# A bottleneck with local self-attention and a bottleneck with a 3x3 convolution: image 0's first 1x1 convolution in seven block products for eight

## The chip, the cores and the metric

The kernel runs on one core of a Trainium2 chip. The metric is device time in microseconds (us); the time given is the median of three runs. A separate execution is recorded by the hardware profiler. Five engines run their own instruction streams and meet at semaphores: TensorE (PE, with its weight loads PEld), VectorE (DVE), ScalarE (ACT), GpSimd (POOL) and SyncE (SP). SP, ACT and POOL also issue DMA transfers.

## The reference

Two residual blocks on x of 16 images, 1024 channels, 32x32 pixels, all in f32:

```
h = relu(bn(conv1x1(x, w_conv1)))                 # 1024 -> 256 channels
q, k, v = relu(bn(wq h)), relu(bn(wk h)), bn(wv h)
attn = softmax over the 9 neighbours of  q . (unfold3x3(k) + pos_h + pos_w)   # 32 heads of 8 channels
h = relu(bn(sum over 9 neighbours of attn * unfold3x3(v)))
x = relu(bn(conv1x1(h, w_conv3)) + x)             # 256 -> 1024, residual
y = relu(bn(conv1x1(x, w1)));  y = relu(bn(conv3x3(y, w2)))
out = relu(bn(conv1x1(y, w3)) + x)
```

The batch norms of the second block have means and variances; those of the first are a scale and a bias.

## The kernel before

An image is 8 chunks of 128 channels by 1024 pixels. A PE product multiplies 128x128 weights with 128x512 data (half the pixels) into a PSUM bank; in the profile one such f32 product is two rows. PSUM holds four tiles of two banks ("ps"), handed out in turn, so that a new tile waits for whoever reads the one four tiles earlier.

The stages of PE stand in a list, in order (line 1026): `P0 P1 P2 P3 C4 F0 Q4 V4 F1 P5 P6 F2 P7 F3 C8 Q8 W0 V8 ...`. C is an image's first convolution (`first_conv`), Q its queries and keys with the position products, V its values (P is C, Q and V in a row), F the fused second half of the first block with the first convolution of the second, W a 3x3 convolution of four images in Winograd form, U and S the last convolution. S, for the last four images, already uses seven block products for eight (`change`, `Quad`, `late_weights`).

- **First convolution** (`first_conv`, `reduce_part`, L389): for each of eight chunks, four products (two output halves by two pixel halves) are summed in two PSUM tiles; two ACT instructions (L1095) then make the hidden tile h. Weights w1 come in two pieces of 512 KB, through `more_weights`.
- **Loads of x** (`more_loads`, L361): image 0's chunk 0 comes in two halves on ACT's queue, chunk 1 also on ACT's; all else on POOL's queue. An x tile is freed, and a later one loaded into it, when its products are done.
- **Projection** (`project`): a key k or a value v is written by ACT (L488) into the padded tile kp, and SP stores it to DRAM (L500), in stage Q or V, at the place in SP's order where it is computed. q goes to DRAM on POOL's queue (L548). The position products (L521) are summed in one tile, which ACT copies to `by_offset` (L529) and POOL stores. `relay` loads all of it back with one head in each partition.
- **Side work** (`Side`): a string of words, ORDER, one for each part of a stage, says what is recorded on DVE and ACT beside that part: j a step of an attention, e its exponentials, f a step of other work, m a load of relayed data, a the relu of an attention's result, w the relu of a Winograd result. Engines run in the order recorded.
- **The f work of the opening**: `winograd_weights` makes the 3x3 filters' Winograd form U: for each of two input halves three 128x768 passes on ACT and six on DVE (from the taps g, loaded by `load_taps`, L272), then six "sets" (`along`) of four ACT and six DVE instructions of 128x256, each of which fills a tile u (L283 to L293), stored by SP to uw (L305). u lies in the pool "h", five tiles that the hidden tiles and q share. `scale_weights` multiplies w3 and u3 by their batch norm scales (L255), after `load_scaled` and `scale_rows` have loaded weights and scales on POOL's queue.
- **Winograd stage** (`winograd_conv`, L822): 18 groups of 8 products. Each needs one weight load U on SP's queue (L132, five rooms) and one V load on POOL's queue; V was stored by SP (L787) from DVE's transform of the hidden images.

[...]

## Time and profile before

| | us |
|---|---|
| median of three runs (2362.63 to 2368.56) | 2364.83 |
| the profiled execution | 2362.54 |
| its span | 2360.8 |
| PE busy | 2349.4 |
| DVE busy | 2154.3 |
| ACT busy | 916.6 |
| POOL busy | 490.2 |

The granted PE clock averages 0.999. Image 0's first convolution takes PE from 4.83 to 33.94 us, its Q and V stages end at 57.35, image 1's first convolution at 85.16. Stage W0 begins at 664.81. The DMA engines move 292 GB/s on average and some 400 GB/s in the first 30 us.

To read the profile: a row of PE in order of time gives start, length, what it is and, in brackets, the idle time before it with what ended that. In lists of waits, the numbers are the total, the count and the longest. Matmuls overlap by 0.16 us in their modelled ends, so that a short wait inside a run of rows doesn't show as idle time; it shows in the starts of the runs.

### The profile page before, as it was taken

The page shows a single profiled execution, that of the slowest core. Times are in us where ns is not written, and L with a number is a line of the kernel's source. Part 1 is how long each engine was busy: PE and PEld are TensorE (multiplying, and loading weights), DVE is VectorE, ACT ScalarE, POOL GpSimd, SP SyncE. Part 2 cuts the span into 40 slices and gives each one's busy share as a digit, 9 for nine tenths or more (in the row PEclk, how much of TensorE's full clock was granted, in tenths as well). Part 3 has the DMA queues.
Part 4 walks back from the last instruction along what each step waited for, and adds up shares of the span by engine and source line. Part 5 has one row for each costly group of instructions (what it writes and reads, how often), then busy time and mean ns, then how long its engine had stood idle before and what let it go on. Part 6 is the DMA issues. An engine that isn't in the chain of part 4 may idle for free.

```text
span 2360.8 us, 18840 instructions
## 1 busy us (share of the span) xinstructions
PE 2349.4 (100%) x6252; PEld 1140.7 (48%) x6252; DVE 2154.3 (91%) x1770; ACT 916.6 (39%) x873; POOL 490.2 (21%) x900
## 2 busy tenths in 40 slices
PE   9999999999999999999999999999999999999998
PEld 4444444444475444444466444444467444444844
DVE  4999999999989999999999999999989999976686
ACT  3323342324122574443122574324222464344266
POOL 2212121212121231111121232111111231111132
PEclk9999999999999999999999999999999999999999
DMA  9968687878797998687898998688788996699888
GB/s 365 368 219 301 245 288 250 284 273 271 262 350 248 341 395 304 217 266 231 265 313 271 328 391 318 221 277 290 262 288 272 335 378 241 213 343 313 314 310 294
DMA packets 295568, 691.63 MB, mean 293 GB/s; under 512 B 20784, under 2 KB 165168, under 8 KB 286768
## 3 DMA queue, kind: packets, MB, share of 16 engines
q0 software_dynamic: 119888, 471.14, 54.9%
q1 hardware_dynamic: 174864, 217.93, 28.6%
q10 hardware_dynamic: 720, 1.36, 0.2%
q8 instruction: 50, 0.82, 0.1%
q14 instruction: 46, 0.38, 0.0%
HBM read 415.32 MB, written 275.03 MB: 292 GB/s over the span
## 4 chain that ended last, share of the span: by engine, by line
PE 91%; DVE 5%; DMA 3%; ACT 0%; issue 0%; POOL 0%; SPq 0%; DVEq 0%; ACTq 0%; POOLq 0%
PE ps L389 34%; PE ps L421 31%; PE ps L475 12%; PE ps L822 9%; PE ps L1263 4%; DVE acc L677 1%; DMA uw<-u 1%; DMA g<-in_u2t_dram 1%; DVE acc L695 1%; PE ps L521 1%; DMA v<-v 1%; DVE v L751 0%; DMA V__2_2534<-v 0%; DMA pos<-by_offset 0%; DVE z L848 0%
## 5 line engine op out<-in xcount | busy, mean ns | idle before, releaser
L389 PE MATMUL ps<-result,u 128*128 128x512 f32 x1024 | 457.8, 592 | 0.0
L421 PE MATMUL ps<-a,w 128*128 128x512 f32 x1024 | 457.7, 592 | 0.0
L389 PE MATMUL ps<-x,w 128*128 128x512 f32 x1024 | 442.9, 593 | 1.0 <-DMA x<-in_x_dram 0.9
L677 DVE TENSOR_TENSOR acc<-e,bnv 128x2048 f32<-128x2048 f32 x144 | 327.4, 2283 | 17.8 <-ACT e L659 14.7
L421 PE MATMUL ps<-y,u 128*128 128x512 f32 x768 | 331.1, 592 | 0.0
L620 DVE TENSOR_TENSOR prod<-qc,bnk 128x2048 f32<-128x2048 f32 x144 | 324.0, 2287 | 1.8
L440 ACT ACTIVATE result<-ps,par 128x1024 f32<-128x1024 f32 x128 | 142.4, 1113 | 458.1 <-PE ps L421 391.6
L389 PEld LDWEIGHTS ps<-x,w 128*128 128x128 f32 x1024 | 194.7, 190 | 246.5 <-issue 243.7
L389 PEld LDWEIGHTS ps<-result,u 128*128 128x128 f32 x1024 | 194.4, 190 | 245.3 <-issue 238.1
L421 PEld LDWEIGHTS ps<-a,w 128*128 128x128 f32 x1024 | 194.6, 190 | 244.9 <-issue 243.5
L695 DVE TENSOR_TENSOR acc<-acc 128x2048 f32<-128x2048 f32 x128 | 293.4, 2292 | 4.4
L421 PEld LDWEIGHTS ps<-y,u 128*128 128x128 f32 x768 | 145.9, 190 | 183.3 <-issue 181.0
L475 PE MATMUL ps<-h,wqk 128*128 128x512 f32 x512 | 222.4, 592 | 0.4 <-ACT h L1095 0.4
L441 POOL DMA_DIRECT2D r<-result x128 | 68.7, 537 | 596.6 <-ACT result L440 592.4
L625 DVE TENSOR_TENSOR prod<-prod 128x2048 f32<-128x2048 f32 (+1 forms) x80 | 166.1, 2077 | 2.2
L475 PEld LDWEIGHTS ps<-h,wqk 128*128 128x128 f32 x512 | 97.1, 190 | 123.2 <-issue 111.2
L440 ACT ACTIVATE result<-ps,bn_sh 128x1024 f32<-128x1024 f32 x96 | 106.7, 1112 | 102.5 <-PE ps L421 96.8
L1095 ACT ACTIVATE h<-ps,par 128x1024 f32<-128x1024 f32 x32 | 38.4, 1202 | 260.0 <-PE ps L389 260.0
L412 ACT ACTIVATE ps<-s 128x1024 f32<-128x1024 f32 x128 | 131.2, 1025 | 15.6 <-DMA s<-in_x_dram 13.1
L488 ACT ACTIVATE kp<-ps,par 128x1024 f32<-128x1024 f32 x64 | 77.3, 1209 | 149.5 <-PE ps L475 120.1
L361 POOL DMA_DIRECT2D x<-in_x_dram x126 | 67.0, 533 | 274.2 <-PE ps L389 205.3
L845 ACT ACTIVATE z<-ps 128x1024 f32<-128x1024 f32 x48 | 49.1, 1024 | 179.1 <-PE ps L822 124.4
(372 smaller groups left out, 2653.8 us busy)
## 6 DMA issues: line engine op xcount, KB each, us to landing
s<-in_x_dram POOLq DMA_DIRECT2D x128, 512.0 KB, 5.8
r<-result POOLq DMA_DIRECT2D x128, 512.0 KB, 4.6
x<-in_x_dram POOLq DMA_DIRECT2D x126, 512.0 KB, 5.2
out_dram<-result POOLq DMA_DIRECT2D x125, 512.0 KB, 7.1
r<-r POOLq DMA_DIRECT2D x111, 512.0 KB, 7.4
v<-v SPq DMA_DIRECT2D x96, 408.0 KB, 4.9
U<-uw SPq DMA_DIRECT2D x60, 512.0 KB, 5.2
bnk<-kp SPq DMA_DIRECT2D x32, 680.0 KB, 7.1
```

What stands on the lines that cost most here:

```text
L389: nc.tensor.matmul(ps[n][:, halves(half)], wt[:, c % (NC // 2), n * P : (n + 1) * P], src[:, halves(half)], start=(c == first), stop=(c == ...
L412: nc.scalar.activation(ps, loaded.pop((self.kind, self.b, o)), AF.Identity)
L421: nc.tensor.matmul(self.ahead[o][:, halves(half)], pieces[key][:, n, o % (NC // 2) * P :][:, :P], self.src[:, n, halves(half)], start=Fals ...
L440: nc.scalar.activation(to_, ps, RELU, bias=self.shift(o), scale=1.0)
L475: nc.tensor.matmul(ps[:, halves(half)], pieces[key][:, m, at : at + P], h[:, m, halves(half)], start=(m == 0), stop=(m == NW - 1),)
L488: nc.scalar.activation(dst, src, func, bias=col(f"L0_conv_{name}_b", n), scale=col(f"L0_conv_{name}_s", n),)
L620: nc.vector.tensor_tensor(by_row(t[:, two]), by_row(qc), kc[:, :, i : i + JROWS, j : j + W], ALU.mult)
L625: nc.vector.tensor_add(u[:, :, 0:4], u[:, :, 0:4], u[:, :, 4:8])
L677: nc.vector.tensor_tensor(by_row(dst), rows(e[:, k, :]).unsqueeze(1).to_broadcast([P, HEAD_DIM, JROWS, W]), vc[:, :, i : i + JROWS, j : j ...
L695: nc.vector.tensor_add(acc, acc, t)
L822: nc.tensor.matmul(acc[i][:, at, :, n, :], pieces[key][:, m, at, n * P : (n + 1) * P], v[:, at, :, m * (TILES + TR) :][:, :, :TILES], star ...
L1263: nc.tensor.matmul(ps, w, by, start=i in (1, 7), stop=True, skip_group_check=True)
```

## The change

Image 0's first convolution runs as `first_conv_of_seven`. Chunks are taken in pairs; with output halves and pixel halves each pair is a 2x2 by 2x2 block product, made with seven products for eight. DVE forms, for each pair, three sums of x halves t1 to t3 in rooms that the attention uses later, and t4 in place of a half of x; and for each piece of w1 four sums of weights s1 to s4 (`sums_of_weights`). The seven results lie in seven PSUM banks of four tiles; `combine` adds them with one ACT copy and seven DVE additions into h, and four ACT relus of 128x512 finish h.

Image 0's x comes as halves, on ACT's and SP's queues, in the order of need, with the first half of the second w1 piece on ACT's queue. Two lent rooms (of tags qc and bnk) hold the u tiles of sets 2 and 3. In `at_first`, four chunks of x go ahead of the second piece of w1; batch norms and the position table follow part 6 of the convolution, `load_scaled` its part 1, `scale_rows` the start of image 0's V stage. ORDER has the f steps of the opening later, the first attention's steps accordingly, and five pairs or so of single steps exchanged later on (the attention's steps in W0 among them).

SP's stores of k are recorded in a list (`put_off`) and issued at once, except in a Q stage followed by W0, which is image 8's: there they go out after part 3 of W0.

```diff
@@ more_weights
         if of[1] == 0 and name == "w1":
-            for part in (slice(0, 1), slice(1, k)) if half == 0 else (slice(0, k),):
-                nc.sync.dma_start(view[:, part], src[:, part])
+            for part, by in (
+                ((slice(0, 2), nc.scalar), (slice(2, k), nc.sync))
+                if half
+                else ((slice(0, 1), nc.sync), (slice(1, k), nc.sync))
+            ):
+                by.dma_start(view[:, part], src[:, part])
@@ winograd_weights
+        lent_rooms = {2: ("qc", JPIX), 3: ("bnk", HALO)}
+
         def along(m, i, row):
-            t = hpool.tile([P, 2 * HW], F32, tag="h", name="u")[:, : NI * WID]
+            if 6 * m + i in lent_rooms:
+                tag, width = lent_rooms[6 * m + i]
+                t = apool.tile([P, HEAD_DIM, width], F32, tag=tag, name="u").rearrange("p d w -> p (d w)")
+            else:
+                t = hpool.tile([P, 2 * HW], F32, tag="h", name="u")
+            t = t[:, : NI * WID]
@@ more_loads
-            by = nc.scalar if loads[0] in (("x", 0, 0), ("x", 0, 1)) else nc.gpsimd
-            for part in (halves(0), halves(1)) if loads[0] == ("x", 0, 0) else (slice(None),):
-                by.dma_start(t[:, part], src[:, part])
+            if (kind, b) == ("x", 0):
+                for part, by in ((halves(0), nc.scalar), (halves(1), nc.sync if c else nc.scalar)):
+                    by.dma_start(t[:, part], src[:, part])
+            else:
+                nc.gpsimd.dma_start(t, src)
@@ project, halo
-                nc.sync.dma_start(
-                    room[n], AP(block.tensor, block.offset, [block.ap[0], [JROWS * PW, NJ], [1, HALO]])
-                )
+                block = AP(block.tensor, block.offset, [block.ap[0], [JROWS * PW, NJ], [1, HALO]])
+                put_off.append(lambda to=room[n], block=block: nc.sync.dma_start(to, block))
+                if name != "bnk" or not stages[now[0] + 1 : now[0] + 2] or stages[now[0] + 1][:2] != FIRST_WINO:
+                    catch_up()
@@ new functions
+    def sums_of_weights(half):
+        s = weight_sums["all"]
+        a = pieces[piece("w1", half)].rearrange("p (q m) (n o) -> p m n q o", m=2, o=P)
+        s1, s2, s3, s4 = (s[:, i, 2 * half : 2 * half + 2] for i in range(4))
+        a11, a12, a21, a22 = a[:, 0, 0], a[:, 1, 0], a[:, 0, 1], a[:, 1, 1]
+        nc.vector.tensor_tensor(s1, a21, a22, ALU.add)
+        nc.vector.tensor_tensor(s2, s1, a11, ALU.subtract)
+        nc.vector.tensor_tensor(s4, a12, s2, ALU.subtract)
+        nc.vector.tensor_tensor(s3, a11, a21, ALU.subtract)
+    def first_conv_of_seven(b):
...
+            nc.vector.tensor_tensor(t1, one[:, halves(1)], one[:, halves(0)], ALU.subtract)
+            if pair % 2 == 0:
+                sums_of_weights(pair // 2)
+            by[1] = a[:, 0, :P], one[:, halves(0)]
+            by[5] = sums_of(0), t1
+            product(1)
+            if pair < last:
+                product(5)
+            yield
+            two = loaded.pop(("x", b, 2 * pair + 1))
+            t4 = one[:, halves(1)]
+            nc.vector.tensor_tensor(t2, two[:, halves(1)], t1, ALU.subtract)
+            nc.vector.tensor_tensor(t3, two[:, halves(1)], t4, ALU.subtract)
+            nc.vector.tensor_tensor(t4, t2, two[:, halves(0)], ALU.subtract)
+            by[2] = a[:, 1, :P], two[:, halves(0)]
+            by[3] = sums_of(3), two[:, halves(1)]
+            by[4] = a[:, 1, P:], t4
+            by[6], by[7] = (sums_of(1), t2), (sums_of(2), t3)
+            for i in (2, 3, 6, 7, 4) if pair < last else (2, 6, 5, 3, 7, 4):
+                product(i)
...
+    def combine(b, banks):
+        h = hidden[b] = hpool.tile([P, NW, HW], F32, tag="h", name=f"h_{b}")
+        c11, c12, c21, c22 = (h[:, n, halves(half)] for n in range(NW) for half in range(2))
+        p1 = u2 = u3 = c22
...
+        nc.scalar.activation(p1, banks[1], AF.Identity)
+        nc.vector.tensor_tensor(c11, banks[2], p1, ALU.add)
+        relu(0, 0, c11)
+        nc.vector.tensor_tensor(u2, banks[6], p1, ALU.add)
+        nc.vector.tensor_tensor(c12, banks[5], u2, ALU.add)
+        nc.vector.tensor_tensor(c12, banks[3], c12, ALU.add)
+        relu(0, 1, c12)
+        nc.vector.tensor_tensor(u3, banks[7], u2, ALU.add)
+        nc.vector.tensor_tensor(c21, u3, banks[4], ALU.subtract)
+        relu(1, 0, c21)
+        nc.vector.tensor_tensor(c22, banks[5], u3, ALU.add)
+        relu(1, 1, c22)
@@ at_first
         warm_up()
         more_weights()
+        more_loads(4)
+        more_weights()
         more_loads()
         nc.scalar.dma_start(par, params)
         more_weights()
-        norms()
         load_taps(0)
-        more_weights()
         load_taps(1)
         more_weights()
         member_table()
         nc.gpsimd.memset(kp, 0.0)
-        load_scaled()
-        scale_rows()
-        position_table()
+        hooks["conv1", 0, 1] = load_scaled
+        hooks["wino", 0, 3] = catch_up
+
+        def prepare():
+            norms()
+            position_table()
+
+        hooks["conv1", 0, 6] = prepare
+        hooks["v", 0, 0] = scale_rows
```

## The prediction

> **What bounds the kernel now.** I read the page first, then TensorE's (PE's) own waits, then its instructions in order of time over the first 110 us, then the chain of waits, and last the DMA issues of the sync engine (SP) around the only large wait.

> ```profile
> span 2360.8 us, 18840 instructions
> PE 2349.4 (100%) x6252; PEld 1140.7 (48%) x6252; DVE 2154.3 (91%) x1770; ACT 916.6 (39%) x873; POOL 490.2 (21%) x900
> ```

> PE is busy all but 11.4 us of the span, so a change can win only by giving PE fewer products or by removing some of its waits. PE's waits, longest in total first (engine and line, what it waited for, us in total, times, longest):

> ```profile
> PE ps L822 <- DMA V__2_2534<-v: 1.5, 1, 1.5
> ...
> PE ps L822 <- issue: 1.0, 1, 1.0
> PE ps L389 <- DMA x<-in_x_dram: 0.9, 1, 0.9
> PE ps L475 <- ACT h L1095: 0.4, 1, 0.4
> ```

> Some waits don't show there, because the ends of matmuls are modelled. They show in PE's rows in order of time (start, length):

> ```profile
> 4.83 3.95 PE L389 MATMUL ps<-x,w 128*128 128x512 f32 x8
> 9.67 24.27 PE L389 MATMUL ps<-x,w 128*128 128x512 f32 x56 [0.89 <-DMA x<-in_x_dram]
> 34.30 14.00 PE L475 MATMUL ps<-h,wqk 128*128 128x512 f32 x32 [0.36 <-ACT h L1095]
> 48.27 2.18 PE L521 MATMUL ps<-q,pos 64*32 64x512 f32 x16
> 50.38 7.13 PE L475 MATMUL ps<-h,wv 128*128 128x512 f32 x16
> 57.35 27.97 PE L389 MATMUL ps<-x,w 128*128 128x512 f32 x64
> 85.16 13.90 PE L475 MATMUL ps<-h,wqk 128*128 128x512 f32 x32
> ```

> Two rows are one product of the program. Undisturbed, 64 rows take 27.47 us (later stages in the chain of waits), so a product costs 27.47/32 = 0.858 us. Image 0's first convolution took 34.30 - 4.83 = 29.47 us for 32 products: 2.0 us of it is waiting. Next, 34.30 to 57.35 is 23.05 us, while the same work undisturbed is 13.73 + 1.02 + 6.97 = 21.72: 1.33 us went at the position products, whose queries (q) left ACT late. Image 1's convolution took 85.16 - 57.35 = 27.81, that is 0.34 us of waiting. The chain of waits says for what:

> ```profile
> 40.57 17.04 DMA uw<-u
> ...
> 58.35 0.92 ACT by_offset L529
> 59.31 26.02 PE ps L389 x60
> ```

> The second sum of image 1 needs the PSUM tile that by_offset (L529) empties, and by_offset stood on ACT behind the filter transform, which waited for its stores uw<-u. VectorE (DVE) waits 14.7 us for those stores in the first 80 us and is then busy over 98% of nearly every stretch up to 660 us.

> **Products.** 28 for 32 in image 0: -4 x 0.858 = -3.43 us of PE work.

> **When the first convolution ends.** Before, image 0's second half-chunk landed about 5.65 us (PE waited for it until 5.72), while three queues moved data; after, two queues hold only what image 0 needs, in order. ACT's first two halves (0.52 MB) with as much from SP are 1.05 MB, and the DMA windows (0.55 MB by 4 us, then 0.41 MB per us) give 5.2 us. I take 5.5. The second product needs t1 (128x512 SBUF add on DVE, 0.69 us in the last stage's rows) and s1 (128x256, 0.42 us): 5.5 + 0.1 + 0.69 + 0.05 + 0.42, with 0.2 to load weights, is 6.95 us. Chunk 1 completes at 1.57 MB, 6.5 to 6.9 us, and t2, t3, t4 at 8.85, 9.55, 10.25 lie ahead of their products (9.5, 10.4, 11.25). From then on data lead: all 5.24 MB are in by 16 us. T = 6.95 + 27 x 0.858 = 30.1 us, between 29.6 (no wait beyond the halves) and 31.5 (chunk 1 at 8 us). [...] The trace: three queues together moved 391 to 414 GB/s from 4 us on. [...]

> The DVE adds 16 x 0.69 + 8 x 0.42 + 7 x 0.69 = 19.2 us in 31 instructions. They lie in 5.5 to 31.7 us, where DVE was idle until 21.05 save for norms (3.2 us, now within the third pair, 5 us ahead of its use). The final sums run between the last products: the last two relus (0.69 us on ACT) end at T + 1.55 and T + 2.3, and the key product needs them at T + 1.72 and T + 2.57. So the 0.36 us wait goes, and the next stage starts at 30.2 for 34.30: **-4.1 us**.

> **What comes late after it.** The filter transform starts on DVE at 31.7 instead of 21.05 (on ACT, 18.7), and by_offset is still behind five of its sets on ACT. A set takes 2.65 us (DVE rows 27.30, 29.95). On ACT the order is now: both q, sets 1 to 3, the second key (1.2 us), sets 4 and 5, three 128x768 passes (0.75 us apart), by_offset. Counting from T: the second q leaves ACT at 11.7, set 1 runs on DVE from 12.2, set 5 from 22.8, its last ACT step ends at 23.2, the passes at 25.5, by_offset at 26.5. Image 1's second sum wants its tile at 0.1 + 21.72 + 1.72 = 23.5. PE waits **3.0 us**, where it lost 1.67 before (1.33 + 0.34): +1.3. From the other side: if ACT ran without these hold-ups the wait would be 0, and each us of a late uw store in set 4 or 5 adds one. The lent rooms make that unlikely: set 4 needs the store of set 0, issued at 40.7 and due at 50; it took 12 us before, with image 1's x still loading. Image 1's convolution thus ends 4.1 - 1.3 = 2.8 us sooner.

> **The rest of the opening.** The w3/u3 loads, row and scales move behind later steps on POOL: the loads behind pair 0's end (about 11.3 us, two x loads first), row/scales behind pc's load. The four scale products on DVE follow the first logits. Logits start at about T + 46.8 = 76.9 (before 81.4, after a transform ending 79.5); scales are needed at 81.4 and should land near 82, hidden or up to 3 us of DVE. DVE then stands 0 to 3 us ahead of before. Its next hold, the tree of L641 at 575.88, waited 2.79 us for by_offset of a later image, so small lateness vanishes there. The attention of image 1 has about 3.5 us to spare before PE's 309.8. par, the taps and wqk go behind x on SP: wqk is used at 30.2, the taps at 31.7, and by 0.4 MB per us (shared with POOL) they are in by 23. Cost 0; uncovered, each us late is one of PE.

> **The put-off stores.** SP in order of time around PE's longest wait:

> ```profile
> 654.84 0.59 SPq L500 DMA_DIRECT2D bnk<-kp  x1
> 655.52 0.55 SPq L132 DMA_DIRECT2D U<-uw  x1
> 665.13 0.36 SPq L500 DMA_DIRECT2D bnk<-kp  x1
> 665.59 22.32 SPq L132 DMA_DIRECT2D U<-uw  x7
> ```

> The second store waited 9.0 us for ACT, and behind it stood the weight load for the fifth group of products, whose 14.7 us end at 680.29; PE went on at 680.41 instead of 678.89. The page blames a V load, but that V belongs to the next group. After the change the weight load goes out as soon as the 16 key/query products end (before: 663.8), 1.7 us sooner, with 1.39 MB (3.5 us at 0.4 MB per us) less ahead. It would land near 676: **-1.5 us**, bounds 0 and -1.5. The stores now stand before the ninth weight load, which is issued near 679, took 12.0 us and is used at 694.3 (692.8 after): the same bytes are ahead of it as before, and 1.9 us are left. No V write of image 8 comes before 733. The later shuffles of single steps (two relus, one vh, one pair of logits) are hidden: they move ACT or DVE work between neighbours of the same stage. Cost 0; uncovered, one step of 1 to 4.5 us.

> **Sum.** -4.1 + 1.3 - 1.5 = **-4.3 us**. The profiled run took 2362.54 (span 2360.8 and 1.7 around it), 2.3 under the median of 2364.83; its like would be 2358.2, and against the median **2360.5 us**. The bound between change and none, 0.3%, is 7.1 us.

> **Rivals.**
> - *by_offset isn't late* (image 1's convolution keeps no wait). For: ACT is busy under half of that stretch. Against: my step-by-step count. Then -4.1 - 1.67 - 1.5 = -7.3: 2357.5.
> - *The put-off is worth nothing:* the next group waits instead. For: the following V load (issued 670.64) also landed near 680.3, and its weights at 682.96 against a need of 682.4. Against: the bytes ahead are gone. -2.8: 2362.0.
> - *DVE becomes the bound:* the four-deep ring of u rooms waits for its stores, and scales are late. DVE has nothing to spare from 80 to 660 us, so lateness reaches PE as soon as the cushions (2.8 us at L641, 3.5 before image 1's attention) are spent. For: 9.4 MB of u stores in 36 us, beside 8 MB of others, are 0.48 MB per us, above the 0.4 seen. It decides when the logits start 11 us later than before, at 92: about +7, 2372.

> **How the numbers follow.** Likeliest 0.45 (2358.5 to 2362.5), by_offset in time 0.30, put-off worthless 0.15, DVE late 0.10. Of the second, 0.27 lie beyond 7.1 us; of the last, 0.07. So faster 0.27, same 0.66, slower 0.07. The range, 2355.5 to 2367, takes in the first three with a measurement's 2 us, and small lateness of DVE.

> **What would show it.** PE's key products starting near 30.2; a gap of about 3 us soon after image 1's convolution begins (near 52), released by by_offset; logits at 77 to 80; no wait at the fifth group of the first Winograd stage. Wrong if PE waits in pairs 0 to 3, if DVE's waits for uw exceed 10 us, or if a new wait appears at 310 us.

## The result

The kernel after the change takes 2361.51 us in the median of 22 executions (2358.49 to 2363.45), the kernel before 2364.82 us (22 executions, beside it). The ratio is 0.9986, with a 95% interval of 0.998 to 0.9992: 3.3 us faster, within the 0.3% that the prediction called no change. The two profiled executions are equal (2362.54 before, 2362.59 after): the one of before lies 2.3 us under its median, the one of after 1.1 above. So the first question to the traces is where the 4.7 us that this execution had won by 52 us went again.

The page of the kernel after, its span and busy times:

```profile
span 2360.9 us, 18891 instructions
PE 2346.8 (99%) x6244; PEld 1139.6 (48%) x6244; DVE 2172.5 (92%) x1801; ACT 917.9 (39%) x876; POOL 487.2 (21%) x894
```

PE is busy 2.6 us less, not the 3.43 of four products: a slower stretch, below, is counted as busy. PE's waits after (what it waited for, us in total, times, longest):

```profile
PE ps L402 <- ACT by_offset L548: 2.7, 1, 2.7
PE ps L842 <- issue: 2.5, 1, 2.5
...
PE ps L842 <- DMA U<-uw: 1.1, 1, 1.1
PE ps L493 <- ACT h L1182: 0.3, 1, 0.3
PE ps L1142 <- DVE bnk L1115: 0.2, 1, 0.2
```

The waits for x and for V__2 are gone. Four others are new or longer. PE in order of time (start, length; idle time before in brackets); L1142 is a product of the seven, L402 is the old L389, L493 the old L475, L842 the old L822:

```profile
4.83 1.83 PE L1142 MATMUL ps<-x,w 128*128 128x512 f32 x2
6.83 1.12 PE L1142 MATMUL ps<-qc,bnk 128*128 128x512 f32 x2 [0.18 <-DVE bnk L1115]
...
30.11 2.06 PE L493 MATMUL ps<-h,wqk 128*128 128x512 f32 x4
32.45 12.28 PE L493 MATMUL ps<-h,wqk 128*128 128x512 f32 x28 [0.27 <-ACT h L1182]
...
52.65 1.88 PE L402 MATMUL ps<-x,w 128*128 128x512 f32 x4
57.18 27.71 PE L402 MATMUL ps<-x,w 128*128 128x512 f32 x60 [2.65 <-ACT by_offset L548]
84.73 13.90 PE L493 MATMUL ps<-h,wqk 128*128 128x512 f32 x32
```

Read against the rows of before: the key products start at 30.11 for 34.30 (-4.19), image 1's convolution at 52.65 for 57.35 (-4.70), but it ends at 84.73 for 85.16 (-0.43). Of the 4.27 lost in it against before, 2.81 are the wait for by_offset (the 2.65 of the row and the 0.16 by which modelled ends overlap). ACT makes that copy right behind the passes of the filter transform:

```profile
55.39 0.83 ACT L295 ACTIVATE g<-g 128x768 f32<-128x768 f32 x1
56.13 1.00 ACT L548 ACTIVATE by_offset<-ps 128x1024 f32<-128x1024 f32 x1
```

Another 1.80 are lost in the 60 rows behind the wait, which take 27.55 us (84.73 - 57.18) where 60 undisturbed rows take 25.75; before, image 1's convolution lost 0.34 in all. The windows of that stretch show why (busy time of PE, PEld, DVE, ACT, POOL with their counts, then the granted PE clock, the DMA share and GB/s):

```profile
56.00:58.00 2.00, 0.82 (x2) 0.53 (x3) 1.90 (x3) 2.00 (x6) 0.58 (x1) 0.91 1.08 293
58.00:60.00 2.00, 2.00 (x3) 0.78 (x3) 1.86 (x3) 0.35 (x2) 2.00 (x5) 0.50 1.07 415
60.00:62.00 2.00, 2.00 (x5) 0.73 (x4) 1.91 (x4) 0.00 (x0) 1.39 (x3) 0.74 1.08 268
62.00:64.00 2.00, 2.00 (x6) 0.94 (x5) 1.83 (x6) 0.46 (x2) 1.01 (x2) 1.00 0.81 311
```

The granted clock is 0.50 from 57.64 to 61.06 us: PE counts as busy, but the windows hold 3 and 5 rows in 2 us instead of 6. That costs half of 3.4 us, 1.7.

The 0.43 us stays until stage W0, which begins at 664.37 for 664.81. There and in W12, the last Winograd stage:

```profile
678.29 3.62 PE L842 MATMUL ps<-V__2_2504,U 128*128 128x256 f32 x16
...
693.32 3.69 PE L842 MATMUL ps<-V__1_2630,U 128*128 128x256 f32 x16 [1.05 <-DMA U<-uw]
...
2182.68 3.62 PE L842 MATMUL ps<-V__0_8347,U 128*128 128x256 f32 x16
...
2202.63 3.69 PE L842 MATMUL ps<-V__2_8425,kp 128*128 128x256 f32 x16 [2.52 <-issue]
```

The fifth group of W0 waits no more (1.52 before), the ninth now waits 1.05. From the first Winograd product to image 8's v products are 63.56 us (727.93 - 664.37) for 64.54. W12 begins 1.56 us sooner (2182.68 for 2184.24), but its sixth group starts at 2202.63 for 2202.69: it waited 2.52 for 1.02. "Issue" hides what it waited for: its V load was issued at 2190.99 and took 11.5 us to land, so at 2202.5; before, 2192.86 and 9.7, also near 2202.5. There what was left of this execution's gain was given back. The sync engine's queue (SP) around W0:

```profile
653.93 21.42 SPq L136 DMA_DIRECT2D U<-uw  x6
675.45 1.22 SPq L519 DMA_DIRECT2D bnk<-kp  x2
678.49 18.88 SPq L136 DMA_DIRECT2D U<-uw  x6
```

The put-off stores go out at 675.45, between the weight loads.

### The profile page after: what moved, and what is told of

Same layout as the page of the kernel before. It is cut to its first block, busy times and chain, and to the rows that moved or that the text cites. A ratio compares the mean times of both kernels' runs of the same rounds, so it can differ in the third digit from the quotient of the medians.

```text
span 2360.9 us, 18891 instructions
## 1 busy us (share of the span) xinstructions
PE 2346.8 (99%) x6244; PEld 1139.6 (48%) x6244; DVE 2172.5 (92%) x1801; ACT 917.9 (39%) x876; POOL 487.2 (21%) x894
## 4 chain that ended last, share of the span: by engine, by line
PE 98%; DMA 1%; DVE 0%; ACT 0%; issue 0%; ACTq 0%; DVEq 0%
PE ps L402 36%; PE ps L434 33%; PE ps L493 14%; PE ps L842 10%; PE ps L1379 4%; PE ps L1142 1%; PE ps L540 1%; DMA U<-uw 1%; DMA x<-in_x_dram 0%; DVE u L294 0%; DVE u L291 0%; ACT g L288 0%; DVE g L292 0%; ACT g L287 0%; ACT result L1409 0%
## 5 line engine op out<-in xcount | busy, mean ns | idle before, releaser
L402 PE MATMUL ps<-result,u 128*128 128x512 f32 x1024 | 457.8, 592 | 0.0
L402 PE MATMUL ps<-x,w 128*128 128x512 f32 x960 | 416.4, 594 | 2.7 <-ACT by_offset L548 2.7
L402 PEld LDWEIGHTS ps<-result,u 128*128 128x128 f32 x1024 | 194.4, 190 | 245.1 <-issue 238.4
L402 PEld LDWEIGHTS ps<-x,w 128*128 128x128 f32 x960 | 182.9, 191 | 233.7 <-issue 229.7
L493 PE MATMUL ps<-h,wqk 128*128 128x512 f32 x512 | 222.8, 593 | 0.3 <-ACT h L1182 0.3
L493 PEld LDWEIGHTS ps<-h,wqk 128*128 128x128 f32 x512 | 97.0, 190 | 123.4 <-issue 110.5
```

The lines of the kernel that those rows point to most:

```text
L402: nc.tensor.matmul(ps[n][:, halves(half)], wt[:, c % (NC // 2), n * P : (n + 1) * P], src[:, halves(half)], start=(c == first), stop=(c == ...
L493: nc.tensor.matmul(ps[:, halves(half)], pieces[key][:, m, at : at + P], h[:, m, halves(half)], start=(m == 0), stop=(m == NW - 1),)
```

## The experiments

Each kernel was timed beside the kernel before on the same chip; its ratio to that is given with the 95% interval. "The stretch" is that from the first Winograd product of W0 to image 8's v products.

| kernel | median us (n) | ratio to before | image 1's conv. ends | the stretch |
|---|---|---|---|---|
| changed kernel | 2361.51 (22) | 0.9986 (0.998 to 0.9992) | 84.73 | 63.56 |
| the same again | 2361.04 (20) | 0.9982 (0.9975 to 0.9988) | 83.46 | 64.35 |
| offset_early | 2356.24 (5) | 0.9966 (0.9953 to 0.9978) | 80.63 | 63.29 |
| the same again | 2357.37 (6) | 0.9971 (0.996 to 0.9983) | 80.51 | 63.70 |
| half_ahead | 2358.59 (8) | 0.9976 (0.9965 to 0.9986) | 82.70 | 65.24 |
| two_ahead | 2358.5 (20) | 0.9975 (0.9969 to 0.9982) | 81.62 | 62.97 |
| late_copy | 2364.76 (12) | 0.9997 (0.9989 to 1.0006) | 87.00 | 66.71 |
| eight | 2362.24 (13) | 0.9993 (0.9985 to 1.0001) | 86.71 | 62.26 |
| early_eight | 2358.32 (12) | 0.998 (0.9972 to 0.9989) | 82.83 | 62.60 |
| no_put_off | 2363.95 (12) | 0.9996 (0.9987 to 1.0004) | 83.69 | 67.05 |
| stores_later | 2360.77 (18) | 0.9983 (0.9976 to 0.999) | 84.75 | 64.34 |
| early_act_stores | 2364.87 (21) | 1.0003 (0.9997 to 1.001) | 80.56 | 70.98 |
| early_w12_queue | 2360.99 (21) | 0.9987 (0.998 to 0.9993) | 80.49 | 65.02 |

(Where the next row begins with a wait for the relu, as in the second offset_early, the end is that row's start less the wait.)

**1. by_offset's copy ahead of the filter transform's passes.**

```diff
@@ ORDER, the words of image 0's C and Q
-        ". . . . . . . f f . fff fff fff . . . ...
+        ". . . . . . . f f . fff . ffffff . . . ...
```

> The changed kernel with the three passes that the word before k's second half's step of image 0 holds moved one word on, so that ScalarE copies image 0's position products (by_offset) right after k's second normalization instead of behind those passes. Nothing is left out. Theory 1 (a late copy stops TensorE for 2.7 us, and the stop of TensorE itself brings its clock to half): the copy ends near 47 instead of 57.1, the wait of 2.7 us at image 1's third product is gone, no stretch of 2 us between 52 and 82 has a granted clock under 0.95, the 60 rows after the wait take 25.75 instead of 27.55 us, and image 1's convolution ends near 80.3 instead of 84.7 (2.65 + 1.8 sooner). Theory 2 (the half clock near 58 to 62 has another cause[...]): the wait goes but the half clock stays, and the convolution ends near 82.1. For the end: if all is kept, 4.4 us less than the changed kernel (ratio to the kernel before near 0.9967); if the sixth group of image 12's Winograd products starts at 2202.6 again, as it did in both profiles, nothing is kept.

ACT's row, PE's row, and the windows of offset_early:

```profile
50.24 1.01 ACT L548 ACTIVATE by_offset<-ps 128x1024 f32<-128x1024 f32 x1
```

```profile
53.16 27.63 PE L402 MATMUL ps<-x,w 128*128 128x512 f32 x64
80.63 13.90 PE L493 MATMUL ps<-h,wqk 128*128 128x512 f32 x32
```

```profile
58.00:60.00 2.00, 2.00 (x6) 0.83 (x5) 1.97 (x3) 0.46 (x2) 0.56 (x1) 1.00 1.09 305
60.00:62.00 2.00, 2.00 (x6) 0.95 (x5) 1.90 (x3) 0.00 (x0) 0.00 (x0) 1.00 0.99 319
```

The copy ends at 51.25 (not 47, since the transform's sets still stand ahead of it), before image 1's convolution begins. The wait is gone, and with it the half clock: all 64 rows take 27.47 us, and the convolution ends 4.1 us sooner though it began 0.5 later. Theory 2 falls: much the same transfers and ACT work pass at that time at full clock. The median is 5.3 us under the changed kernel's, which was timed apart from it; by the two ratios to the kernel before it is 4.7 (0.9966 against 0.9986). Since that rested on five executions, it was run again beside the changed kernel:

> The kernel with by_offset's copy early once more, since its first time rests on five executions. Nothing is left out. Theory: 2356 to 2358 in the median, 4 to 5 us under the changed kernel beside it; no half clock in image 1's convolution, which ends near 80.3. Rival (the first five were lucky): 2358.5 or more.

> The changed kernel once more, for a second profile. Nothing is left out. The wait for by_offset is 2.6 to 2.7 us again; if the half clock follows, image 1's convolution ends near 84.7, if not (as in one of four profiles with a wait of this size) near 83.0. The wait at image 12's sixth group, 2.5 us in the first profile of this kernel, is by my account a matter of the single execution (0 to 2.5 us over the profiles so far) and comes out differently. Time 2361 to 2362.

2357.37 against 2361.04, 3.7 us less in the median and 2.6 by the ratios. These two kernels differ only in where one word's passes stand, and this version beats both the kernel before and the changed one. The changed kernel's second profile waits as long as the first, without the half clock, and W12's wait comes out differently, 1.82:

```profile
57.61 26.02 PE L402 MATMUL ps<-x,w 128*128 128x512 f32 x60 [2.65 <-ACT by_offset L548]
...
2201.45 3.69 PE L842 MATMUL ps<-V__2_8425,kp 128*128 128x256 f32 x16 [1.82 <-issue]
```

**2. How long a stop must be.** In two_ahead and half_ahead PE has other products to do while by_offset is late; in late_copy the copy is made later still. The first part of the diff gives the order of the products in words.

```diff
@@ first_conv, for image 1: chunks 0 and 1
-  c0: sum 0, sum 1;  c1: sum 0, sum 1
+  two_ahead:   c0: sum 0;  c1: sum 0;          c0: sum 1;  c1: sum 1
+  half_ahead:  c0: sum 0;  c1: half of sum 0;  c0: sum 1;  c1: rest of sum 0, sum 1
@@ positions, for late_copy
-            nc.scalar.activation(by_offset, ps, AF.Identity)
+            for _ in range(3 if b == 0 else 1):
+                nc.scalar.activation(by_offset, ps, AF.Identity)
```

> The changed kernel with image 1's first convolution in another order: the first sum's products of chunks 0 and 1, then the second sum's of both, so that two more products (0.86 us) stand before the one that waits for by_offset, which stays as late as it was. Nothing is left out. TensorE's wait becomes 1.8 us. Theory 1a (the clock falls only after a longer stop; the stop of 1.5 us in the kernel before left it at 1.00): no half clock, and image 1's convolution ends near 82.1 (0.86 + 1.8 sooner than 84.7). Theory 1b (any stop here brings the half clock): a stretch at 0.5 follows as before, and it ends near 83.9.

> The changed kernel with one more of image 1's first-sum products (128x512, 0.86 us) ahead of the product that waits for by_offset, which stays as late as it was. Nothing is left out. The wait becomes 1.8 us, between the stops that left the clock at 1.00 (up to 1.5 us) and the shortest after which it was seen at a half (2.0 us). If 1.8 us are too short for it: no half clock, and image 1's convolution ends near 82.1. If not: a stretch at 0.5 follows and it ends near 83.9.

> The changed kernel with image 0's copy of by_offset done three times over (two idle copies of some 0.9 us ahead of the one that counts), so that TensorE's wait becomes 2.65 + 1.9 = 4.5 us. Nothing is left out. Theory (a stop of TensorE brings one stretch of half clock of fixed length): about 3.5 us at 0.5 follow, as after the shorter wait, and image 1's convolution ends near 86.6, 1.9 us later than in the changed kernel's profile. Rival (the loss grows with the stop, or the stretch has to do with the transfers or ScalarE's work of that moment and not with the stop): it ends at 87.5 or later, or near 84.8 without a half clock.

```profile
57.48 3.70 PE L1202 MATMUL ps<-x,w 128*128 128x512 f32 x8 [0.93 <-ACT by_offset L548]
...
2198.88 5.38 PE L842 MATMUL ps<-V__2_8425,kp 128*128 128x256 f32 x16 [2.01 <-issue]
```

Those are rows of two_ahead. Its expectation missed the size: two products are 1.72 us, not 0.86, so the wait is 0.93. No half clock follows, and the convolution ends at 81.62, 3.1 us sooner than in the changed kernel's first profile (expected 82.1). But in W12, where nothing was altered, a stop of 2.01 us brought the half clock (16 rows in 5.38 us for 3.69). In half_ahead the wait is 1.79, without half clock; the convolution ends at 82.70 (expected 82.1, and it began 0.5 later). In late_copy:

```profile
59.45 27.71 PE L402 MATMUL ps<-x,w 128*128 128x512 f32 x60 [4.76 <-ACT by_offset L549]
...
698.20 5.38 PE L843 MATMUL ps<-V__1_2632,U 128*128 128x256 f32 x16 [2.52 <-DMA U<-uw]
```

A stop of 4.76 us is followed by one half stretch, from 60.11 to 63.52, no longer than after 2.65; the convolution ends at 87.00 (expected 86.6). So the loss behind this stop is no larger. late_copy's median is 3.7 us above that of the changed kernel beside it, more than these 2.3 (3.5 against that kernel's second profile): its W0 shows 2.52 us of wait and a second half clock.

**3. Seven products or eight.**

```diff
-    FEWER = (0,)
+    FEWER = ()
```

> The changed kernel with image 0's first convolution of eight products again (32 for 28 in all); the loads in their new order, the new order of steps and the put-off stores stay. Nothing is left out. Theory (in the changed kernel the seven products' gain is lost to the late copy of by_offset and to the half clock that its wait brings): the first convolution ends 3.4 to 3.7 us later, near 33.7, image 1's convolution begins near 56.4, the wait for by_offset (which ScalarE gives at 57.1 in any case) shrinks to 0 to 1 us, no half clock follows, and that convolution ends between 83.7 and 85, as in the changed kernel (84.7): the time is the changed kernel's, 2361 to 2362. Rival (the seven products carry the gain of 3.3 us in the median): 2364 to 2365.

> The kernel with by_offset's copy early, with eight products again for seven. Nothing is left out. Theory (with nothing late behind it a product that isn't computed is worth its 0.858 us to the end): 3.4 us, less 0.3 to 0.6 for the last relus that the seven products wait for, over the same kernel with seven: 2359 to 2359.8 in the median. Rival (the end is set elsewhere by then, by the transfers of image 0's and image 12's Winograd stages): within 1 us of the same kernel with seven, 2356 to 2357.

With the changed kernel's order (eight):

```profile
54.56 1.88 PE L402 MATMUL ps<-x,w 128*128 128x512 f32 x4
59.22 27.65 PE L402 MATMUL ps<-x,w 128*128 128x512 f32 x60 [2.78 <-ACT by_offset L548]
86.71 13.90 PE L493 MATMUL ps<-h,wqk 128*128 128x512 f32 x32
```

I had taken by_offset to be late by ACT's work alone. It is not: its copy comes at 58.17 for 56.13, because ACT's chain to it begins behind the queries, which PE delivers later. The wait stays (2.78, with a half clock), so that my theory for this run fell. The products' gain passes through the wait, at 1.98 us (86.71 - 84.73). In time the ratios give 1.7 us (0.9993 against 0.9986), between the theory's nothing and the rival's 3.3; the medians are only 0.7 apart, but the kernel before, beside which each was timed, was itself 1.1 lower in this set. With the early copy, eight products end image 1's convolution 2.2 us later (82.83 for 80.63). The median is 2.1 above that of offset_early; the ratios give 3.3 (0.998 against 0.9966), and 2.1 against the second run (0.9971), so that the 2.8 to 3.1 expected is not excluded.

So four products of 3.43 us are worth some 2 us in the traces and 1.7 to 3.3 by the ratios, and the traces show where the rest stays. Eight products end the first convolution at 33.28 (early_eight) for 30.64 (offset_early), or 32.75 (eight) for 30.11 (changed kernel): 2.64 twice, not 3.43, since with seven the second product waits until its two sums are made (6.83 in the changed kernel), and some 0.8 us more goes at the start than with eight. (The size isn't firm: over the eleven profiles with seven products the key products start between 30.11 and 30.79, and PE's opening rows are slow for a different time: the first two take 1.83 us in the changed kernel, 1.66 in early_act_stores and 1.02 in eight, and early_eight's first 64 take 28.62 us where 64 undisturbed rows take 27.63.) And from there to image 1's convolution are 22.5 us for 21.8: 0.72 more, for the last relus. The rest of the change with eight products, above all the loads in their new order, brings the key products to 32.75 and 33.28 for 34.30: 1.0 to 1.5 us, of which 0.36 is the wait for the relu, which is gone there.

**4. The put-off stores.**

```diff
@@ no_put_off: halo
                 put_off.append(lambda to=room[n], block=block: nc.sync.dma_start(to, block))
-                if name != "bnk" or not stages[...] or stages[...][:2] != FIRST_WINO:
-                    catch_up()
+                catch_up()
@@ stores_later: at_first
-        hooks["wino", 0, 3] = catch_up
+        hooks["wino", 0, 10] = catch_up
@@ early_act_stores (with the early copy): halo, nothing put off
+                first_wino = name == "bnk" and stages[now[0] + 1][:2] == FIRST_WINO
+                (nc.scalar if first_wino else nc.sync).dma_start(room[n], block)
```

> The changed kernel with image 8's k stores issued at once, as before the change. Nothing is left out. My account: the fifth Winograd group waits some 1.5 to 2.1 us again, the ninth waits for nothing, and the stretch from the first Winograd product to image 8's v takes 64.5 us as before the change instead of 63.6: the put-off is worth 1.0 us. Rival (the fifth group's wait went because of everything else that lies some 0.4 us earlier): the fifth group waits 0.5 us or less and the stretch takes 63 us or less.

> The changed kernel with image 8's two put-off k stores issued after the eleventh part of image 0's Winograd products instead of after the fourth. Nothing is left out. Theory (the weights of the ninth group are 1.05 us late because they stand behind these stores): the ninth group waits for nothing, the stretch from the first Winograd product to the first product of image 8's v takes 62.5 us instead of 63.6, and the wait does not come back at a later group. Rival (all transfers together are late there, whatever their order): a wait of about 1 us appears at a later group, 12 to 18, and the stretch stays at 63.6.

> The kernel with by_offset's copy early, with image 8's two k stores not put off but issued at once on ScalarE's queue, so that no weight load stands behind them. Nothing is left out. Theory (the order on the sync engine's queue makes the weights late): neither the fifth nor the ninth Winograd group waits, the stretch from the first Winograd product to image 8's v takes 62.5 us for the 63.3 of the kernel with the put-off, time 0.8 us less. Rival (the stage is short of transfer as a whole, so that any 1.4 MB in it cost a wait): a wait of 0.5 to 2 us stays at one of the groups and the stretch is 63 us or more.

no_put_off, PE:

```profile
57.84 26.02 PE L402 MATMUL ps<-x,w 128*128 128x512 f32 x60 [2.65 <-ACT by_offset L547]
...
681.24 5.36 PE L841 MATMUL ps<-V__2_2504,U 128*128 128x256 f32 x16 [2.88 <-DMA U<-uw]
```

The fifth group waits 2.88 us, for the weights, as the prediction had read it (the page of before had named a V load), and a half clock of 1.7 us follows: the stretch is 67.05 us. Without the put-off the changed kernel can't be told from the one before (0.9996, interval 0.9987 to 1.0004). The put-off is thus worth 2.4 us in the median, more than the 1.0 that the two first profiles showed; in this profile the longer wait brings 1.7 us of half clock besides. stores_later, PE, and then the window from 710 to 720 us in the changed kernel and in stores_later:

```profile
718.29 3.69 PE L842 MATMUL ps<-V__1_2752,U 128*128 128x256 f32 x16 [1.37 <-DMA U<-uw]
```

```profile
710.00:720.00 10.00, 10.00 (x48) 8.80 (x47) 9.71 (x11) 3.07 (x3) 1.59 (x3) 1.00 0.78 269
710.00:720.00 10.00, 8.63 (x41) 7.32 (x40) 9.76 (x12) 3.07 (x3) 1.58 (x3) 1.00 1.02 407
```

The ninth group's wait is gone and the sixteenth waits 1.37: the stretch is 64.34, so the theory that the stage gains when the two stores go elsewhere in the queue falls, and the rival holds in this profile: the late stores fill a stretch of the DMA engines that had room (a busy share of 0.78 in the changed kernel, 1.02 here). Over the whole stretch the DMA engines are busy for 0.96 of the time in the changed kernel and 0.99 here, so that there is little to spare; but it is 0.97 in eight too, which waits for nothing there. That a full stage must wait is therefore not shown, only that these stores cost a wait wherever they were put. The ratio, 0.9983, can't be told from the changed kernel's. early_act_stores is the clearest failure: 8.6 us slower than offset_early. GpSimd's queue, ACT and PE of it:

```profile
664.68 0.53 POOL L374 DMA_DIRECT2D V__2_2504<-v  x1 [13.71 <-PE ps L841]
665.20 1.53 POOL L566 DMA_DIRECT2D q<-q  x2
666.72 0.71 POOL L551 DMA_DIRECT2D pos<-by_offset  x1
667.42 2.14 POOL L557 DMA_DIRECT2D pos<-by_offset  x4
```

```profile
679.89 1.02 ACT L864 ACTIVATE z<-ps 128x1024 f32<-128x1024 f32 x1 [11.06 <-DMA pos<-by_offset]
```

```profile
680.97 5.88 PE L841 MATMUL ps<-V__2_2504,U 128*128 128x256 f32 x16 [6.29 <-ACT z L864]
```

The load of V's fifth group goes out at 664.68 instead of 659.20 (offset_early), and behind it on the same queue the stores of by_offset, which land after 679. ACT's third copy z takes the room that by_offset held, so it waits 11 us for those stores, and the fifth group waits 6.29 for the PSUM tile that this copy empties. Why the V load goes out 5.5 us later can be read from the landings: it waits for the last of SP's six v stores (v<-v), which was issued at 649.93 and took 14.2 us, so it landed at 664.1; in offset_early it was issued at 649.41 and took 9.2, so it landed at 658.6. The first of the two k stores, on ACT's queue from 650.63, was under way beside it and landed at 663.9, after 13.3 us. So the k store, though no weight load stood behind it, ran beside a transfer of another queue that then took 5.0 us longer.

**5. W12's stores on another queue.**

```diff
@@ Expand.result
-            nc.gpsimd.dma_start(to, t)
+            (nc.scalar if self.b == 11 and 2 <= o <= 4 and self.kind == "r" else nc.gpsimd).dma_start(to, t)
```

> The kernel with by_offset's copy early, with the three last result stores of image 11 ahead of image 12's Winograd stage issued on ScalarE's queue when they are computed, instead of on GpSimd's queue, where they wait for 10 us behind the load of V's fifth group and then stand before that of the sixth. Nothing is left out. Theory (the sixth group waits because its V load is behind these 1.6 MB on its queue): the V load of the sixth group is issued 1.6 us sooner and lands 3 us sooner, the group's wait (0.5 in this kernel's profile, 1.0 and 2.5 in those before and after the change) is gone, 0 to 1 us less. Rival (the transfers of that stretch are late as a whole): the wait stays, or the stores delay the shuffles v<-v and the fifth group waits.

```profile
2196.32 3.69 PE L842 MATMUL ps<-V__2_8378,kp 128*128 128x256 f32 x16 [1.93 <-DMA V__2_8378<-v]
2199.85 3.62 PE L842 MATMUL ps<-V__2_8425,kp 128*128 128x256 f32 x16
```

The sixth group's wait is gone, and the fifth waits 1.93: its load went out 10.8 us after W12's start (2191.21 - 2180.42) instead of 4.75 (2183.07 - 2178.32), since the shuffles v<-v that it waits for were later. The rival describes this profile, though a wait here differs from one profile to the next (below). In the median it is 4.8 us above offset_early and 3.6 above its second run, of which the profile shows 1.5 in W12 and 1.7 in W0, where the two kernels are the same; the rest isn't explained.

## Why the prediction was right, point by point

- **When the first convolution ends.** Right: second product at 6.83 (6.95 was worked out), key products at 30.11 (30.2), -4.19 us for -4.1; this profile is the earliest of eleven, the latest has 30.79. The split was off: with eight products the rest of the change brings 1.0 to 1.5, the seven products 2.64. DVE's first sum, which waits for x's second half, began at 5.75 (6.17 and 5.85 in the second profiles of the changed kernel and offset_early), no sooner than the 5.72 until which PE waited for that half before: so for that half the two queues brought nothing, and what the loads brought came with the later chunks. The DMA engines moved 407 GB/s from 4 to 8 us before and 389 after.
- **"The last two relus ... need them at T + 1.72 and T + 2.57. So the 0.36 us wait goes."** Wrong. The relus took 0.81 us for 0.69 and were held by DVE's final sums; the first of the last two ended at 32.39, where T + 1.72 is 31.83, and the rows from 30.11 to 44.66 are 14.55 us for 13.83. A term of +0.7 was missing.

```profile
31.58 1.54 ACT L1182 ACTIVATE h<-h,par 128x512 f32<-128x512 f32 x2 [0.58 <-DVE h L1194]
```

- **by_offset late, a wait of 3.0 us.** Right: 2.65, by the mechanism counted (sets and passes ahead of it on ACT). What failed is the price, "+1.3": a stop of PE was priced at its length. In three of the five profiles with this wait (changed kernel, stores_later, eight; not no_put_off, not the changed kernel again) 1.7 us of half clock followed; which it is depends on where the stop falls, as the last section shows. "Image 1's convolution thus ends 2.8 us sooner" measured 0.43 with the half clock and 1.70 without.
- **The rival that by_offset isn't late** (2357.5): offset_early makes that case, and took 2356.24 and 2357.37. The rival's number was right, in part by luck: image 1's convolution ends 4.5 to 4.7 us sooner than before there, not the 5.8 that the rival adds up to (4.1 + 1.67), and the put-off gave more.
- **The put-off, -1.5 us.** That the stores held the fifth group's weights is shown (no_put_off), and in the medians the put-off is worth 2.4. **"1.9 us are left"** for the ninth weight load is wrong: it was 1.05 and 1.84 us late in the two profiles of the changed kernel. The bytes ahead of it had been counted as the same as before; which of them came later isn't known.
- **The rival that the next group waits instead** (2362.0). In the two profiles of the changed kernel it comes close: a wait of 1.05 and 1.84 us at the ninth group for 1.52 at the fifth, and a stretch only 0.98 and 0.19 us shorter than before. Its number is even nearer to 2361.51 (by 0.5) than the 2360.5 of the sum (by 1.0). Against it stands no_put_off alone, where the stretch is 2.7 to 3.5 us longer and the median 2.4 higher.
- **VectorE as the bound, the scales, the tail's shuffles at 0.** The first two did not come about: in the first 700 us DVE waits for no uw store (14.7 us before), and the logits begin at 77.61 (76.9 was worked out). The tail's moved steps did nothing that shows, but the tail isn't neutral: W12's sixth group waits between 0 and 2.5 us over the profiles (1.02 before; 2.52 and 1.82 in the changed kernel's two; 0.45 and 0 in offset_early's; 0.79 in early_eight but 2.51 in eight, 0 in no_put_off). Two profiles of one kernel differ by 0.5 to 0.7 us; whether the rest belongs to the kernels or to the single execution isn't known. A single profile can thus hide much of a gain of 2 us, and this one did.

The sum of -4.3 stands against -3.3 in the medians of the first set (-3.3 by the ratio) and -3.5 in those of the second (-4.3 by the ratio). That it is so near is in part luck: the half clock and the relus, which had no price, made the forecast gain too large, and a put-off that was worth more made up for part of it.

## What to carry to other kernels

Where an engine was given less work ahead of a copy that another engine makes late, look for that copy first: moving it one word in the order ended image 1's convolution 3.0 to 4.1 us sooner (2.6 and 4.7 us of the time by the ratios), where the four products themselves gave 2.0 to 2.2 (1.7 to 3.3). Price a stop of PE at its length plus, where it is as long as those here that a half clock followed (2.01 us and more), 1.7 us times the chance that it falls badly (three of the five stops of 2.6 to 2.8 us at by_offset). In a stage where the DMA engines are busy for 0.96 of the time, ask of every transfer that is moved what it will run beside: none of the four places and queues tried here for such stores was without a wait behind it, though the put-off paid all the same. Fewer bytes in the stage were not tried.

## What was not expected of the hardware

| profile, stop | idle in the window(s) | next window |
|---|---|---|
| changed kernel, 54.53 to 57.18 | 2.65 | half |
| stores_later, 54.73 to 57.37 | 2.33 | half |
| changed kernel again, 54.96 to 57.61 | 2.65 in all; without a half stretch its grid isn't placed | full |
| kernel before, 678.89 to 680.41 | 1.52 | full |
| late_copy, 54.69 to 59.45 | 2.01, then 2.75 | full, then half |
| two_ahead, 2196.87 to 2198.88 | 2.01 | half |
| no_put_off, 55.19 to 57.84 | 1.39, then 1.26 | full, full |
| changed kernel, 2200.11 to 2202.63 | 1.11, then 1.41 | full, full |
| early_act_stores, 674.68 to 680.97 | 3.41, then 2.43 | half, half |

In these stops a window with 1.52 us of idle time or less was followed by a full one and a window with 2.33 or more by a half one; 2.01 was followed by a full one in late_copy and by a half one in two_ahead. So the edge lies near 2.0 us here; the ends of matmuls are modelled, and it isn't known to a tenth. A stop of 2.65 us cost nothing beyond its length where a boundary split it near the middle, as in no_put_off. An estimate from these figures: of 3.41 us of places for the boundary, 1.37 leave both parts under 2.01, so that such a stop falls badly in 0.6 of cases (it was three of five) and costs 1.0 us more than its length on average. The prediction priced its wait of 3.0 us at its length alone; the profile of before, whose longest stop behind the opening is 1.52 us, shows no half clock behind a stop.

Left open: with eight products PE has no listed wait in W0 (stretches of 62.26 and 62.60 us), with seven and the same put-off it always has 0.5 to 2.5 us of it, though the DMA engines are as busy (0.97 and 0.96); what of the first convolution reaches so far was not tried.
